# A two-layer graph network: edge tiles loaded and stored in pairs, and the copies into PSUM placed one by one in the step

## The chip, the cores and the metric

The kernel runs on one core of one Trainium2 chip. A core has five engines with instruction streams of their own: TensorE (PE in the profile, PEld for its weight loads), VectorE (DVE), ScalarE (ACT), GpSimd (POOL) and SyncE (SP). Each works through its stream in order and waits on semaphores for the others. Data goes between memory and the core's SBUF through DMA queues; here SyncE issues the plain loads and stores, and GpSimd issues gathers by row number. The metric is the device time of one launch in microseconds (us). The times given are medians of a few runs; beside them stands one execution taken by the hardware profiler.

## The reference

There are 6250 nodes and 106250 edges with vectors of D = 256 float32 numbers. The edges are sorted by their destination `dst`. Two layers follow each other, each one wrapped in a residual and a layer normalisation:

```python
# layer 0
msg = relu(x[src] + edge_attr)
h   = x + x + segment_sum(msg, dst)
f   = gelu(bn1(h) @ W1.T + b1) @ W2.T + b2
x   = layernorm(x + bn2(h + f))
# layer 1
m   = gelu((x[src] + edge_attr) @ W1m + b1m) @ W2m + b2m
agg = segment_sum(m, dst) / max(degree, 1)
u   = gelu(agg @ W1u + b1u) @ W2u + b2u
x   = layernorm(x + layernorm(x + u))
```

The BatchNorms `bn1` and `bn2` use given means and variances.

## The kernel before

**What is computed when.** The product in layer 1 is split: (x[src] + edge) @ W1m is proj[src] + edge @ W1m, with proj = x @ W1m + b1m made per node at the end of layer 0. Layer 1 so gathers rows of proj where layer 0 gathers rows of x. The edges stand in 831 tiles of 128, eight tiles make a span, and a span has two groups of four tiles; there are V = 104 spans. In layer 1 all edge tiles have to be multiplied by W1m. For group 1 this is done in layer 1 itself. For group 0 it is done ahead, in layer 0, and the products z go to a buffer `zst` in memory, from which layer 1 loads them.

**The steps.** The program is one long list in an order written out by hand (`manual_schedule`), so each engine's stream is what the text of the program says, in that order. It has one step for each span v. While span v is gathered, span u = v-1 gets its edges added, span w = v-2 is summed into slots, and span v-3 (`full`) is added into node blocks. A step of layer 0 (`step_0`) has:

- `load_0(v+3)`: one load of the eight edge tiles of a span (1 MB, L774), and the node rows xb when a block begins (L1049);
- `gather`: eight indirect DMAs (L791) on GpSimd, one for each tile, into `ring[v % 5]`, the room that the span five before had; a gather waits until that span's slot sums (L874) have read the room;
- `turned`, twice: two edge tiles of group 0 are transposed on TensorE (L804) into a PSUM buffer `workP`, and ScalarE copies them to SBUF as `eaT` (L809);
- `one_hots(u)`: eight small comparisons on VectorE (L852);
- `full_0`: sums over slots are multiplied into the accumulators of the node blocks (L902), and the degrees are made (L910 on TensorE, L915 on VectorE);
- `activated(w, 1)`: the activation of group 1 on ScalarE (L843);
- `lifted` and `add_to_gathered`, four times: ScalarE copies two edge tiles from SBUF to a `workP` buffer (L828, called the lift here), and VectorE adds them to the gathered rows in the ring (L835);
- two `product`s (L817), each of two tiles by W1m; VectorE copies them to `z` (L1098 and L1107), and one store of 512 KB takes both to `zst` (L1108);
- `slot_nodes` (L861), `into_slots` (L874, TensorE: the sums over 32 slots into the one buffer `slotP`) and `kept_slots` (L883, ScalarE);
- one phase each of the node work that is under way (`advance`), the oldest block early in the step, the others at its end.

A step of layer 1 (`step_1`) is the same in build. It loads 512 KB of `zst` (L1226) and 512 KB of edges (L774) ahead, and x1 and degrees of a block when it begins; it transposes and multiplies group 1 of span u, adds these products from PSUM (L835), and lifts and adds the two pairs of group 0. When a node block begins, `full_1` first makes an opening one-hot on VectorE (L896), for which L902 waits. The node work of layer 1 is `nodes_1` (L1161 on TensorE, L1166 on VectorE, L1171 on ScalarE, L1188, L1198 and L1202, and the store L1210).

**Buffers.** There are four `workP` buffers, taken in turn by every transposition, lift and product, whichever engine fills them; a new use waits until the use four before has been read. The pool `edges` has four buffers `ea` of a whole span, and two of `z`. `slotP` has one buffer, which L915 reads last. The order of a layer-0 step before, in uses of `workP`: transpose 1, transpose 2, lift and add 1, lift and add 2, product 1, lift and add 3, lift and add 4, product 2. In layer 1: transpose 1, transpose 2, lift and add 1, lift and add 2, product 1 (added: the third add), product 2 (the fourth add).

Of the kernel before, what the change touches and what calls it, by code (L numbers as in the profile page):

```python
# [14 lines left out]
P = 128  # L15
D = 256
# [486 lines left out]
def kernel(  # L503
# [76 lines left out]
    zst = dram.tile([len(window), P, G * D], F32, name="zst")  # L580
# [52 lines left out]
    with (  # L633
        tc.tile_pool(name="check", bufs=1) as check,
        tc.tile_pool(name="state", bufs=1) as state,
        tc.tile_pool(name="edges", bufs=AHEAD + 1) as ep,
# [132 lines left out]
        def load_edges(v, some, to):  # L769

            counts = sum((tiles_of(v, g) for g in some), [])
            for j, k, n in runs(counts):
                r0 = (v * SPAN + some[0] * G + j) * P
                nc.sync.dma_start(  # L774
                    out=to[:n, j:k, :],
                    in_=edge_attr[r0 : r0 + (k - j - 1) * P + n, :].rearrange(
                        "(j p) d -> p j d", p=n
                    ),
                )

        def edge_tiles(v):
            ea = ep.tile([P, SPAN, D], F32, name="ea")
            for g in range(GROUPS):
                eas[v, g] = ea[:, g * G : (g + 1) * G, :]
            return ea
# [12 lines left out]
        def turned(v, g, q, ea):  # L798

            pair = tiles_of(v, g)[q : q + 2]  # L800
            pe = work().rearrange("p j (k e) -> p j k e", k=KC)
            for j, n in enumerate(pair):
                for k in range(KC):
                    nc.tensor.transpose(  # L804
                        pe[:, j, k, :n], ea[:n, q + j, k * P : (k + 1) * P], ident[:n, :n]
                    )
# [16 lines left out]
        def lifted(v, g, q, of):  # L823

            pair = tiles_of(v, g)[q : q + 2]
            ps = work()
            for j, k, n in runs(pair):
                nc.scalar.copy(ps[:n, j:k, :], of[:n, q + j : q + k, :])  # L828
# [212 lines left out]
        eas, xbs, acc, degs = {}, {}, {}, {}  # L1041

        def load_0(v):
            load_edges(v, range(GROUPS), edge_tiles(v))
# [30 lines left out]
        zs = {}  # L1075

        def step_0(v):
# [3 lines left out]
            if v < V:  # L1081
                gather(v, x)
                first = turned(v, 0, 0, eas[v, 0])
                second = turned(v, 0, 2, eas[v, 0])
                zs[v] = ep.tile([P, G, D], F32, name="z", bufs=2)
# [7 lines left out]
            if 0 <= u < V:  # L1093
                add_to_gathered(u, 0, 0, lifted(u, 0, 0, eas[u, 0]))
                add_to_gathered(u, 0, 2, lifted(u, 0, 2, eas[u, 0]))
            advance(early)
            if v < V:
                nc.vector.tensor_copy(zs[v][:, 0:2, :], product(*first))  # L1098
            if 0 <= u < V:
                for q in range(0, len(tiles_of(u, 1)), 2):  # L1100
                    add_to_gathered(u, 1, q, lifted(u, 1, q, eas[u, 1]))
                activated(u, 0, AF.Relu)
            if 0 <= w < V:
                slot_nodes(w)
                kept_slots(w, into_slots(w, D + 1))
            if v < V:
                nc.vector.tensor_copy(zs[v][:, 2:4, :], product(*second))  # L1107
                nc.sync.dma_start(out=zst[v], in_=zs.pop(v).rearrange("p j d -> p (j d)"))  # L1108
# [105 lines left out]
        def load_1(v):  # L1214
# [10 lines left out]
            edge_tiles(v)  # L1225
            nc.sync.dma_start(out=eas[v, 0].rearrange("p j d -> p (j d)"), in_=zst[v])  # L1226
            load_edges(v, [1], eas[v, 1])
# [9 lines left out]
        def step_1(v):  # L1237
# [5 lines left out]
            some = 0 <= u < V  # L1243
            if some:
                first = turned(u, 1, 0, eas[u, 1])
                second = turned(u, 1, 2, eas[u, 1])
# [4 lines left out]
            if 0 <= w < V:  # L1251
                activated(w, 1, AF.Gelu)
            if some:
                add_to_gathered(u, 0, 0, lifted(u, 0, 0, eas[u, 0]))
                add_to_gathered(u, 0, 2, lifted(u, 0, 2, eas[u, 0]))
# [12 lines left out]
        for v in range(AHEAD):  # L1268
            load_0(v)
# [7 lines left out]
        for v in range(AHEAD):  # L1277
            load_1(v)
# [66 lines left out]
```

## Time and profile before

| what | value |
|---|---|
| median of 3 runs | 2827.88 us (2816.51 to 2832.43) |
| profiled execution | 2846.84 us |
| its span on the core | 2845.0 us |
| mean granted TensorE clock | 0.869 of full speed |
| layer 0: first to last gather | about 5 to 1304 us |
| layer 1: first to last step | about 1440 to 2790 us |
| bytes through queue q1 (loads and stores of SyncE) | 309.65 MB, 32.3% of 16 engines' span |
| bytes through queue q0 (gathers) | 217.71 MB, 25.1% |

How to read the lines that follow: times are in us unless marked ns. In the groups of instructions a line names the code line, engine, operation, output <- input and the number of instructions; then busy time and mean ns of one; then the idle time of the engine just before them and what ended most of it. In a timeline a line is start, duration, engine, code line and tile names, and in brackets the idle time ahead of it and the releaser ("remote" is a semaphore update of another engine that the profile doesn't trace to one instruction; "issue" is time in which nothing shown was waited for). In the list of waits: who waited <- for what: us in all, times, longest. Matmuls are pipelined and their ends are modelled.

### The profile page before, as it was taken

How to read it: one execution, taken by the hardware profiler on the slowest of the kernel's cores; microseconds unless marked ns; L12 is line 12 of the kernel's file. 1: busy time of each engine (PE TensorE's matmuls, PEld its weight loads, DVE VectorE, ACT ScalarE, POOL GpSimd, SP SyncE). 2: the span in 40 equal slices, each digit the busy share in tenths (PEclk: the TensorE clock that was granted, in tenths of full speed). 3: DMA queues.
4: the chain of work that ended last, by engine and by line, in shares of the span. 5: the costliest groups of instructions: out<-in, count | busy, mean ns of one | idle time of the engine just before them, and what ended most of it. 6: DMA issues, size and time to landing. Idle time of an engine off the chain costs nothing.

```text
span 2845.0 us, 37182 instructions
## 1 busy us (share of the span) xinstructions
PE 2074.6 (73%) x11784; PEld 1530.3 (54%) x11784; DVE 1410.2 (50%) x4130; ACT 1347.7 (47%) x2140; POOL 1579.9 (56%) x1671
## 2 busy tenths in 40 slices
PE   3788887887887787788357766776677677757776
PEld 2556655665665565565235544554555556545554
DVE  3554555555555555555124544455455455545555
ACT  1455555555554554555123544445444454435443
POOL 6556565665656665562455554555555656555540
PEclk7998999999998998998668987888888889878887
DMA  6676676676776776774445554555555555545540
GB/s 213 223 233 218 217 242 215 230 240 206 239 228 209 233 235 214 234 226 157 125 137 163 180 169 140 166 168 172 170 165 183 171 167 188 173 147 165 170 131 14
DMA packets 312069, 531.71 MB, mean 187 GB/s; under 512 B 36325, under 2 KB 231480, under 8 KB 311736
## 3 DMA queue, kind: packets, MB, share of 16 engines
q1 hardware_dynamic: 231416, 309.65, 32.3%
q0 software_dynamic: 79744, 217.71, 25.1%
q8 instruction: 97, 1.59, 0.2%
q10 hardware_dynamic: 704, 1.87, 0.2%
q14 instruction: 108, 0.88, 0.1%
HBM read 455.34 MB, written 73.75 MB: 186 GB/s over the span
## 4 chain that ended last, share of the span: by engine, by line
PE 25%; another core or an unknown queue 12%; issue 7%; DVE 6%; ACT 5%; DMA 2%; POOL 0%; ACTq 0%; DVEq 0%; SPq 0%; POOLq 0%
PE workP L817 10%; PE nodeP L1188 3%; PE slotP L874 3%; PE acc L902 3%; PE workP L804 2%; PE nodeP L1161 2%; DVE ring L835 2%; DMA ring<-proj,src_sb 1%; ACT ring L843 1%; ACT L958 1%; ACT workP L828 1%; DVE hot L852 1%; ACT eaT L809 1%; DVE uT L1166 1%
## 5 line engine op out<-in xcount | busy, mean ns | idle before, releaser
L791 POOL DMA_INDIRECT ring<-proj,src_sb x831 | 789.8, 950 | 671.2 <-issue 303.8
L791 POOL DMA_INDIRECT ring<-in_x_dram,src_sb x831 | 788.2, 949 | 513.3 <-issue 224.0
L817 PE MATMUL workP<-w1m_sb,eaT 128*128 128x256 f32 x3324 | 905.7, 416 | 146.7 <-ACT eaT L809 88.8
L835 DVE TENSOR_TENSOR ring<-workP,ring 128x512 f32<-128x512 f32 x832 | 542.7, 682 | 622.5 <-remote 322.3
L817 PEld LDWEIGHTS workP<-w1m_sb,eaT 128*128 128x128 f32 x3324 | 656.8, 206 | 354.7 <-issue 128.7
L902 PE MATMUL acc<-hot,sums 128*128 128x160 f32 (+19 forms) x1360 | 264.5, 332 | 303.3 <-DVE hot L896 169.2
L843 ACT ACTIVATE ring<-ring 128x1024 f32<-128x1024 f32 x418 | 441.9, 1058 | 75.8 <-DVE ring L835 65.2
L902 PEld LDWEIGHTS acc<-hot,sums 128*128 128x128 f32 x1360 | 210.8, 217 | 343.1 <-DVE hot L896 125.2
L828 ACT COPY workP<-ea 128x512 f32<-128x512 f32 x624 | 344.2, 595 | 93.7 <-DVE ring L835 62.1
L883 ACT COPY sums<-slotP 128x257 f32<-128x257 f32 (+1 forms) x208 | 76.9, 370 | 641.0 <-remote 324.5
L804 PE MATMUL workP<-ident,ea 128*128 128x128 f32 x1662 | 258.0, 293 | 158.5 <-DVE z L1098 105.6
L809 ACT COPY eaT<-workP 128x512 f32<-128x512 f32 x416 | 228.9, 585 | 296.2 <-PE workP L804 148.0
L874 PE MATMUL slotP<-ring,hot 128*32 128x257 f32 (+1 forms) x3324 | 265.5, 402 | 91.5 <-remote 40.3
L804 PEld LDWEIGHTS workP<-ident,ea 128*128 128x128 f32 x1662 | 205.4, 150 | 222.2 <-DVE z L1098 131.1
L852 DVE TENSOR_SCALAR hot<-ramp,slot 128x32 f32<-128x32 f32 x1662 | 265.8, 257 | 0.0
L874 PEld LDWEIGHTS slotP<-ring,hot 128*32 128x32 f32 x3324 | 108.5, 112 | 221.6 <-issue 105.5
L1098 DVE COPY z<-workP 128x512 f32<-128x512 f32 x104 | 71.3, 685 | 201.2 <-remote 128.0
L1171 ACT ACTIVATE uT<-uT,cols_sb 128x256 f32<-128x256 f32 (+1 forms) x100 | 44.9, 495 | 255.9 <-DVE uT L1166 214.0
L915 DVE TENSOR_TENSOR degs<-degs,slotP 1x160 f32<-1x160 f32 (+24 forms) x170 | 36.4, 241 | 226.8 <-issue 69.6
L1161 PE MATMUL nodeP<-fT,w 128*128 128x256 f32 (+1 forms) x400 | 105.6, 408 | 23.3 <-issue 11.6
L1188 PE MATMUL nodeP<-w2u_sb,uT 128*128 128x256 f32 (+1 forms) x392 | 106.1, 432 | 5.8 <-DVE y L1202 5.0
L1161 PEld LDWEIGHTS nodeP<-fT,w 128*128 128x128 f32 x400 | 80.6, 209 | 43.8 <-issue 21.3
(112 smaller groups left out, 1466.2 us busy)
## 6 DMA issues: line engine op xcount, KB each, us to landing
ea<-in_edge_attr_dram SPq DMA_DIRECT2D x103, 1024.0 KB
zst<-z SPq DMA_DIRECT2D x104, 512.0 KB
ea<-zst SPq DMA_DIRECT2D x104, 512.0 KB
ea<-in_edge_attr_dram SPq DMA_DIRECT2D x103, 512.0 KB
ring<-in_x_dram,src_sb POOLq DMA_INDIRECT x831
ring<-proj,src_sb POOLq DMA_INDIRECT x831
xb<-in_x_dram SPq DMA_DIRECT2D x24, 256.0 KB
x1d<-x SPq DMA_DIRECT2D x24, 256.0 KB
```

Of the source, the lines that this page charges most:

```text
L791: nc.gpsimd.indirect_dma_start(out=rings[v % RING][:n, g * G + j, :D], out_offset=None, in_=table, in_offset=bass.IndirectOffsetOnAxis(ap= ...
L804: nc.tensor.transpose(pe[:, j, k, :n], ea[:n, q + j, k * P : (k + 1) * P], ident[:n, :n])
L809: nc.scalar.copy(eaT[:, j:k, :, :n], pe[:, j:k, :, :n])
L817: nc.tensor.matmul(ph[:n, j, :], lhsT=eaT[:, j, k, :n], rhs=w1m_sb[:, k, :], start=(k == 0), stop=(k == KC - 1),)
L828: nc.scalar.copy(ps[:n, j:k, :], of[:n, q + j : q + k, :])
L835: nc.vector.tensor_add(r[:n, at + j : at + k, :D], ps[:n, j:k, :], r[:n, at + j : at + k, :D])
L843: nc.scalar.activation(at, at, func)
L852: nc.vector.tensor_scalar(hots[v][:n, j, :], ramp[:n, :SLOTS], slot[:n, t : t + 1], None, op0=ALU.is_equal,)
L874: nc.tensor.matmul(ps[q * SLOTS : (q + 1) * SLOTS, :width], lhsT=hot[:n, j, :], rhs=r[:n, j, :width], start=(i == 0), stop=(i == PAIR - 1 ...
L902: nc.tensor.matmul(acc[b][:, k, cols], lhsT=its[:, k * P : (k + 1) * P], rhs=at, start=(begins and k == 0), stop=(last_span[b] == v and k ...
L1161: nc.tensor.matmul(ps[:, o - i, :width], lhsT=w12[:, k, o * P : (o + 1) * P], rhs=mT[:, k, :width], start=(k == 0), stop=(k == KC - 1),)
L1188: nc.tensor.matmul(ps[:n, h, :], lhsT=uT[:, k, h * P : h * P + n], rhs=w2u_sb[:, k, :], start=(k == 0), stop=(k == UC - 1),)
```

## The change

Edge tiles are handled in pairs throughout. The pool `edges` has 16 buffers of two tiles where it had four of eight, and `z` has four of two tiles where it had two of four. A load is one pair (256 KB), and in layer 0 each of the two products is stored by itself as soon as it is copied (256 KB; `zst` is laid out for that). The load of a pair is issued right behind the lift that frees a pair's room, four spans ahead (`raised`), where before a whole span was loaded at the head of the step, three spans ahead. At the start of both layers four spans are loaded ahead, not three.

The lifts and their adds are moved. In layer 0 the order in uses of `workP` is now: transpose 1, lift and add 1, transpose 2, lift and add 2, product 1, lift and add 3, lift and add 4, product 2; the one-hots come after the first add, the second lift after `activated(w, 1)`, the third behind the first product, and the fourth behind `activated(u, 0)`. In layer 1: transpose 1, lift and add 1, transpose 2, lift and add 2, product 1, product 2. What is computed stays the same.

```diff
--- before.py
+++ after.py
@@ -577,7 +577,7 @@
     proj = dram.tile([N, D], F32, name="proj")
     x1d = dram.tile([N, D], F32, name="x1d")
     degd = dram.tile([1, N], F32, name="degd")
-    zst = dram.tile([len(window), P, G * D], F32, name="zst")
+    zst = dram.tile([len(window), G // 2, P, 2 * D], F32, name="zst")
 
     c.update(
         ident=ident, ones=ones, eps=eps, col=col, row=row, src_sb=src_sb, dstf=dstf,
@@ -633,7 +633,7 @@
     with (
         tc.tile_pool(name="check", bufs=1) as check,
         tc.tile_pool(name="state", bufs=1) as state,
-        tc.tile_pool(name="edges", bufs=AHEAD + 1) as ep,
+        tc.tile_pool(name="edges", bufs=(AHEAD + 1) * SPAN // 2) as ep,
         tc.tile_pool(name="hots", bufs=2) as hp,
         tc.tile_pool(name="nodes", bufs=2) as npool,
         tc.tile_pool(name="accP", bufs=2, space=bass.MemoryType.PSUM) as psa,
@@ -766,23 +766,27 @@
             nc.sync.dma_start(out=b2m_col, in_=b2m.rearrange("o (k p) -> p (o k)", p=P))
 
 
-        def load_edges(v, some, to):
-
-            counts = sum((tiles_of(v, g) for g in some), [])
-            for j, k, n in runs(counts):
-                r0 = (v * SPAN + some[0] * G + j) * P
+        eas = {}
+        HALVES = [(g, q) for g in range(GROUPS) for q in range(0, G, 2)]
+
+        def edge_tile(v, g, q):
+            eas[v, g, q] = ep.tile([P, 2, D], F32, name="ea")
+            return eas[v, g, q]
+
+        def load_edges(v, g, q):
+
+            pair = tiles_of(v, g)[q : q + 2]
+            if v >= V or not pair:
+                return
+            to = edge_tile(v, g, q)
+            for j, k, n in runs(pair):
+                r0 = (v * SPAN + g * G + q + j) * P
                 nc.sync.dma_start(
                     out=to[:n, j:k, :],
                     in_=edge_attr[r0 : r0 + (k - j - 1) * P + n, :].rearrange(
                         "(j p) d -> p j d", p=n
                     ),
                 )
-
-        def edge_tiles(v):
-            ea = ep.tile([P, SPAN, D], F32, name="ea")
-            for g in range(GROUPS):
-                eas[v, g] = ea[:, g * G : (g + 1) * G, :]
-            return ea
 
         def gather(v, table):
             for g in range(GROUPS):
@@ -795,14 +799,15 @@
                         in_offset=bass.IndirectOffsetOnAxis(ap=src_sb[:n, t : t + 1], axis=0),
                     )
 
-        def turned(v, g, q, ea):
-
+        def turned(v, g, q):
+
+            ea = eas[v, g, q]
             pair = tiles_of(v, g)[q : q + 2]
             pe = work().rearrange("p j (k e) -> p j k e", k=KC)
             for j, n in enumerate(pair):
                 for k in range(KC):
                     nc.tensor.transpose(
-                        pe[:, j, k, :n], ea[:n, q + j, k * P : (k + 1) * P], ident[:n, :n]
+                        pe[:, j, k, :n], ea[:n, j, k * P : (k + 1) * P], ident[:n, :n]
                     )
             eaT = hp.tile([P, 2, KC, P], F32, name="eaT", bufs=3)
             for j, k, n in runs(pair):
@@ -820,12 +825,13 @@
                     )
             return ph
 
-        def lifted(v, g, q, of):
-
+        def lifted(v, g, q):
+
+            of = eas[v, g, q]
             pair = tiles_of(v, g)[q : q + 2]
             ps = work()
             for j, k, n in runs(pair):
-                nc.scalar.copy(ps[:n, j:k, :], of[:n, q + j : q + k, :])
+                nc.scalar.copy(ps[:n, j:k, :], of[:n, j:k, :])
             return ps
 
         def add_to_gathered(v, g, q, ps):
@@ -1038,10 +1044,9 @@
             )
             nc.sync.dma_start(out=rows_of(proj, b), in_=y[:n, :H, :])
 
-        eas, xbs, acc, degs = {}, {}, {}, {}
+        xbs, acc, degs = {}, {}, {}
 
         def load_0(v):
-            load_edges(v, range(GROUPS), edge_tiles(v))
             for b in range(blocks):
                 if first_span[b] == v:
                     _, H, n = shape(b)
@@ -1072,7 +1077,11 @@
             for b in into_blocks(v, acc, opened_0, degs):
                 begun(b, nodes_0(b, acc.pop(b), xbs.pop(b), degs.pop(b)))
 
-        zs = {}
+        def stored(v, q, ps):
+
+            z = ep.tile([P, 2, D], F32, name="z", bufs=4)
+            nc.vector.tensor_copy(z, ps)
+            nc.sync.dma_start(out=zst[v, q // 2], in_=z.rearrange("p j d -> p (j d)"))
 
         def step_0(v):
             u, w, full = v - 1, v - 2, v - 3
@@ -1080,9 +1089,17 @@
                 load_0(v + AHEAD)
             if v < V:
                 gather(v, x)
-                first = turned(v, 0, 0, eas[v, 0])
-                second = turned(v, 0, 2, eas[v, 0])
-                zs[v] = ep.tile([P, G, D], F32, name="z", bufs=2)
+                first = turned(v, 0, 0)
+
+            def raised(g, q):
+
+                if 0 <= u < V and tiles_of(u, g)[q : q + 2]:
+                    add_to_gathered(u, g, q, lifted(u, g, q))
+                    load_edges(u + AHEAD + 1, g, q)
+
+            raised(0, 0)
+            if v < V:
+                second = turned(v, 0, 2)
             if 0 <= u < V:
                 one_hots(u)
             early, late = running[:1], running[1:]
@@ -1090,22 +1107,19 @@
                 full_0(full)
             if 0 <= w < V:
                 activated(w, 1, AF.Relu)
-            if 0 <= u < V:
-                add_to_gathered(u, 0, 0, lifted(u, 0, 0, eas[u, 0]))
-                add_to_gathered(u, 0, 2, lifted(u, 0, 2, eas[u, 0]))
+            raised(0, 2)
             advance(early)
             if v < V:
-                nc.vector.tensor_copy(zs[v][:, 0:2, :], product(*first))
+                stored(v, 0, product(*first))
+            raised(1, 0)
             if 0 <= u < V:
-                for q in range(0, len(tiles_of(u, 1)), 2):
-                    add_to_gathered(u, 1, q, lifted(u, 1, q, eas[u, 1]))
                 activated(u, 0, AF.Relu)
+            raised(1, 2)
             if 0 <= w < V:
                 slot_nodes(w)
                 kept_slots(w, into_slots(w, D + 1))
             if v < V:
-                nc.vector.tensor_copy(zs[v][:, 2:4, :], product(*second))
-                nc.sync.dma_start(out=zst[v], in_=zs.pop(v).rearrange("p j d -> p (j d)"))
+                stored(v, 2, product(*second))
             advance(late)
 
 
@@ -1222,9 +1236,12 @@
                         out=degs_1[b][:, :width],
                         in_=degd[:, b * SB : b * SB + width].to_broadcast([P, width]),
                     )
-            edge_tiles(v)
-            nc.sync.dma_start(out=eas[v, 0].rearrange("p j d -> p (j d)"), in_=zst[v])
-            load_edges(v, [1], eas[v, 1])
+
+        def load_products(v, q):
+            if v < V:
+                nc.sync.dma_start(
+                    out=edge_tile(v, 0, q).rearrange("p j d -> p (j d)"), in_=zst[v, q // 2]
+                )
 
         def opened_1(b):
             acc_1[b] = psa.tile([P, KC, SB], F32, name="acc")
@@ -1241,18 +1258,27 @@
             if v < V:
                 gather(v, proj)
             some = 0 <= u < V
+
+            def raised(q):
+                if some:
+                    add_to_gathered(u, 0, q, lifted(u, 0, q))
+                    load_products(u + AHEAD + 1, q)
+
             if some:
-                first = turned(u, 1, 0, eas[u, 1])
-                second = turned(u, 1, 2, eas[u, 1])
+                first = turned(u, 1, 0)
+            raised(0)
+            if some:
+                load_edges(u + AHEAD + 1, 1, 0)
+                second = turned(u, 1, 2)
                 one_hots(u)
             early, late = running[:1], running[1:]
             if 0 <= full:
                 full_1(full)
             if 0 <= w < V:
                 activated(w, 1, AF.Gelu)
+            raised(2)
             if some:
-                add_to_gathered(u, 0, 0, lifted(u, 0, 0, eas[u, 0]))
-                add_to_gathered(u, 0, 2, lifted(u, 0, 2, eas[u, 0]))
+                load_edges(u + AHEAD + 1, 1, 2)
             advance(early)
             if some:
                 add_to_gathered(u, 1, 0, product(*first))
@@ -1265,8 +1291,11 @@
             advance(late)
 
         begin()
-        for v in range(AHEAD):
-            load_0(v)
+        for v in range(AHEAD + 1):
+            for g, q in HALVES:
+                load_edges(v, g, q)
+            if v < AHEAD:
+                load_0(v)
         load_w(w1t_sb, w1t)
         load_w(w2t_sb, w2t)
         slots_of_edges()
@@ -1274,8 +1303,12 @@
         for v in range(V):
             step_0(v)
             beside.get(v, lambda: None)()
-        for v in range(AHEAD):
-            load_1(v)
+        for v in range(AHEAD + 1):
+            if v < AHEAD:
+                load_1(v)
+            for q in (0, 2):
+                load_products(v, q)
+                load_edges(v, 1, q)
         for v in range(V, V + 3):
             step_0(v)
         finish()
```

## The prediction

> **What bounds the kernel now.** I read the page's busy times first, then the groups of instructions, the list of waits, and the timeline of single steps. All sums are against the profiled execution (2846.84 us, span 2845.0); the three timed runs have a median of 2827.88, 0.7% under it, so a difference found in the one is carried to the other unscaled. From no change, a measurement of this kernel can tell about 0.5% (14 us).
>
> ```profile
> PE 2074.6 (73%) x11784; PEld 1530.3 (54%) x11784; DVE 1410.2 (50%) x4130; ACT 1347.7 (47%) x2140; POOL 1579.9 (56%) x1671
> ...
> L791 POOL DMA_INDIRECT ring<-proj,src_sb x831 | 789.8, 950 | 671.2 <-issue 303.8
> L791 POOL DMA_INDIRECT ring<-in_x_dram,src_sb x831 | 788.2, 949 | 513.3 <-issue 224.0
> ```
>
> No engine is full. POOL issues 8 gathers in a step, 0.95 us each with 0.30 between: 8 x 0.95 + 7 x 0.30 = 9.7 us. Yet the median step, from one copy of the slot sums (L883) to the next, is 12.3 us in layer 0 and 12.2 in layer 1. The timeline of a layer-0 step shows the rest:
>
> ```profile
> 613.12 1.89 PE L817 MATMUL workP<-w1m_sb,eaT 128*128 128x256 f32 x8
> ...
> 614.95 1.08 PE L874 MATMUL slotP<-ring,hot 128*32 128x257 f32 x16
> ...
> 618.45 0.95 POOL L791 DMA_INDIRECT ring<-in_x_dram,src_sb  x1 [0.30 <-issue]
> 620.42 0.69 DVE L1098 COPY z<-workP 128x512 f32<-128x512 f32 x1 [4.84 <-remote]
> ...
> 621.43 0.38 ACT L883 COPY sums<-slotP 128x257 f32<-128x257 f32 x1 [4.16 <-remote]
> 621.86 0.95 POOL L791 DMA_INDIRECT ring<-in_x_dram,src_sb  x1 [2.47 <-ACT sums L883]
> ```
>
> The first product ends at 615.01 and the slot sums at 616.03 by the record, but VectorE and ScalarE move on only at 620.42 and 621.43, after the last gather of the batch ended at 619.40. The next batch starts 2.47 later (median of layer 0: 2.58). This is how the trace has it throughout: what TensorE finishes late in a batch of gathers is seen by the other engines after the batch. Of the degree products (L910) of layer 0, those that ended under 4.5 us after a batch began held VectorE's L915 up by over 1 us in 13 of 56 steps, those that ended later in 35 of 38. So layer 0 is a loop: batch 9.7, gap 2.6, together 12.3. TensorE's own end of the slot sums lies a median 3.2 us before the copy: that is the slack of everything else. In 21% of the steps it is under 0.7.
>
> Layer 1 has a mean step of 13.34 against its median of 12.23. The difference sits in 19 stalls: two batches 0.3 apart, then POOL idle for 9 to 13 us. One of them:
>
> ```profile
> 1824.32 0.95 POOL L791 DMA_INDIRECT ring<-proj,src_sb  x1 [0.30 <-issue]
> 1825.50 0.69 DVE L835 TENSOR_TENSOR ring<-workP,ring 128x512 f32<-128x512 f32 x1 [11.40 <-remote]
> 1828.36 0.87 DVE L1166 SCALAR_TENSOR_TENSOR uT<-degb,b,nodeP 128x256 f32<-128x256 f32 x2 [2.17 <-remote]
> 1828.87 0.91 ACT L1171 ACTIVATE uT<-uT,cols_sb 128x256 f32<-128x256 f32 x2 [12.19 <-DVE uT L1166]
> 1829.15 1.25 DVE L852 TENSOR_SCALAR hot<-ramp,slot 128x32 f32<-128x32 f32 x8
> 1829.68 1.05 ACT L809 COPY eaT<-workP 128x512 f32<-128x512 f32 x2
> 1830.31 0.35 DVE L896 TENSOR_SCALAR hot<-ramp,node_of 128x256 f32<-128x256 f32 x1
> ...
> 1830.71 2.08 PE L902 MATMUL acc<-hot,sums 128*128 128x256 f32 x4 [13.19 <-DVE hot L896]
> ...
> 1836.90 0.94 POOL L791 DMA_INDIRECT ring<-proj,src_sb  x1 [11.64 <-ACT ring L843]
> ```
>
> The slot sums of the step before ended 3.8 us after the earlier batch had begun, early enough to get through, so the next batch followed at once and the second product and L1161 were held over both. In 10 of the 19 stalls a new node block opens (L896 in the gap), and TensorE waits for it:
>
> ```profile
> PE acc L902 <- DVE hot L896: 169.2, 20, 48.2
> ```
>
> **The change, part by part.** *Transfers.* A step of layer 0 has 4 loads and 2 stores of 256 KB for one load of 1 MB and one store of 512 KB; layer 1 has 4 loads of 256 KB for 2 of 512 KB. Bytes are the same, and runs of 2 KB move as fast as those of 4 KB (85 and 177 ns a packet in the trace, 24.0 and 23.2 GB/s an engine). SyncE issues one in 0.33 to 0.47 us:
>
> ```profile
> 607.65 0.37 SPq L774 DMA_DIRECT2D ea<-in_edge_attr_dram  x1
> ...
> 608.47 0.46 SPq L1015 DMA_DIRECT2D x1d<-x  x1
> ```
>
> Six of them are 2.4 us of a 12.3 us step on an engine with nothing else. What landed shows the next price: the 1 MB load issued at 607.65 had moved by 612.80, the 256 KB store issued behind it at 608.47 by 613.62, 0.8 us after it, which is about its own bytes. The Trainium skill, "DMA: Bandwidth & Descriptors" (section "Anatomy of one DMA"), gives each DMA some 2.0 us of fixed cost beside its bytes, and half efficiency at about 860 KB; it fits this on POOL's kind of DMA. That speaks against the change: 4 more DMAs a step are 8 us, 104 x 8 = +832 us in layer 0, if they stood one behind the other on the path. By the row they overlap in the queue; I take the row. And they aren't on the path: an edge tile is loaded 3 to 4 steps (37 to 49 us) ahead of its transpose and lands 2 to 6 us after issue. Even at 10 us late the cover holds. SyncE's queue is now held at each lift, in turn, and the x1d, proj and output stores queue behind it; they have no reader in the same layer. Price 0; without that cover each late load would stop TensorE at L804 for what it is late.
>
> *Start and turn of the layers.* The first tile is there after 256 KB, not 1 MB: TensorE's first transpose, at 13.38 us waiting for this load, may come some 3 us earlier. But the second product copy is at 57.19 because five batches of gathers run to 57. Price 0 (-3 to 0). A fourth span loaded ahead: 0.
>
> *Order, layer 0.* The four workP buffers go round in the order of use. The second transposes (T2) used to wait for the third add of the step before, now for the fourth: 0.68 later on VectorE, and T1 covers a part. After the release VectorE does z copy and two adds, ending 2.0 us later, where T2 could begin at 1.3 to 1.4: +0.55 us for T2, L902, L910, L817. The slack of 3.2 hides it in most steps. Two places don't: L910 ends later, and VectorE's L915 frees the one slotP buffer for L874. Of 94 steps 7 had L910 at 5.5 to 6.0 us after the batch began; those past 6.0 had steps about 1.3 us longer: 7 x 1.3 = +9. If all of it showed, 104 x 0.55 = +57. In return the first add no longer stands behind L915 (0.68 us of VectorE's work in the held steps): a bound of 21% x 104 x 0.68 = -15. I take +8, near the first since the release, not VectorE, ends those waits.
>
> *Order, layer 1, opening steps.* VectorE's first add now comes before the one-hots (L852) and L896, and it needs the first lift, which ScalarE does after the first transposes' copy. In the stall above: L1171 ends 1829.78, copy 0.59 to 1830.24 as now, lift 0.59 to 1830.8, add 0.69 to 1831.4, one-hots to 1832.7, L896 to 1833.0. L902 starts there instead of 1830.71: +2.3 us, and behind it on TensorE stand the product, L874 and, for it, POOL. 10 stalls x 2.3 = +23. Bounds: add alone 0.7 x 10 = 7; all 25 openings, 57. Other steps have 3.9 us of median slack: 0.
>
> *Order, layer 1, other stalls.* T2 now waits for the third add (0.69) that stands at the head after a release: +0.4 for L874. On the path in 9 stalls: +4. But the same 0.4 to 0.6 moves L874's end in the early batches, and 5 of 17 such ends lay at 5.2 to 5.6 us after the batch began; the ones not followed at once start at 5.6. Each stall costs 11.1 (mean idle) - 2.6 (usual gap) - 2.3 (gap saved before) = 6.2 us. Escapes: 0 to 5; I take 2, -12, since ends of 6.1 to 6.9 also got through.
>
> **Sum.** 8 + 23 + 4 - 12 = +23 us, about 0.8%: 2827.88 + 23 = 2851. No engine gains or loses an instruction beside SyncE.
>
> **The rivals.** *The stalls dissolve (faster).* Place: L874 in layer 1 after a short step; the delay of T2, and of activation L843 behind the lift, pushes its release past the early window, and POOL waits as in layer 0, where no batch but one followed at once. For it: ends cluster at 3.6 to 5.7. Against: 7 of the 17 are at 4.2 or less, and 0.6 doesn't carry them over. It decides from about 6 stalls gone (37 against the 35 of the other terms). Half of 19 gone: 9 x -6.2 = -56, the other layer-1 terms halved to 14, layer 0 +8: 2794; all gone: 2718.
>
> *Nothing moves.* The new waits end before the gathers do, the transfers were hidden before and after: 2828. For it: median slacks of 3.2 and 3.9 us. Against: L902's wait for L896 has no slack.
>
> *TensorE's chain becomes the loop.* T2's wait shows in each step: +57 in layer 0, 104 x 0.45 = +47 in layer 1, +23: 2955; a half of it, 2900. Against: steps with slack under 0.7 are a fifth.
>
> **How the numbers follow.** The sum as worked 0.42 (own range 2835 to 2880); stalls dissolve 0.32; nothing moves 0.16; TensorE's chain 0.10. Faster by over 0.5% (under 2813.7): 0.30 + 0.02 = 0.32. Within: 0.05 + 0.02 + 0.11 = 0.18. Slower (over 2842.0): 0.37 + 0.03 + 0.10 = 0.50. Range 2765 to 2900: it takes in the half-dissolved case and half of TensorE's chain.
>
> **What would show it.** Transfers: no wait of L804 or L828 for a DMA; SyncE's waits end at lifts. Layer 0: POOL's gap stays near 2.6 and the step near 12.3; L915's held waits grow. Openings: the wait of L902 for the opening one-hot above 169 us, L902 about 7.3 us after a double batch instead of 5.1. Stalls: their number near 17 to 19. I am wrong if the number of double batches falls below about 13, if gathers cost other than 0.95 us among smaller transfers, or if TensorE is seen waiting for loads.

## The result and the profile after

The changed kernel takes 2912.68 us (median of 4 runs) against 2830.15 for the kernel before: 1.029 times as long, 95% interval 1.0245 to 1.0343. It is slower, as forecast, but by 82 us where 23 were forecast, and 2912.68 lies above the range of 2765 to 2900.

First the groups of GpSimd's gathers (busy us, mean ns of one, then the idle time ahead of them), layer 1 above layer 0. The line L791 is now L795.

```profile
L795 POOL DMA_INDIRECT ring<-proj,src_sb x831 | 791.3, 952 | 682.0 <-issue 379.2
L795 POOL DMA_INDIRECT ring<-in_x_dram,src_sb x831 | 789.3, 950 | 563.9 <-issue 349.0
```

A gather costs what it did. GpSimd's idle time has grown by 51 us in layer 0 (513.3 before) and by 11 in layer 1 (671.2). Counted by steps, the time from the first to the last copy of slot sums is 1320 us in layer 0 (1269 before) and 1376 in layer 1 (1357): +51 and +19. The prediction had +8 and +15. The step of layer 0 has a median of 13.3 us, up from 12.3.

The groups of instructions name the place. Of the changed kernel (L921 is the degree add, L880 the slot sums):

```profile
L921 DVE TENSOR_TENSOR degs<-degs,slotP 1x160 f32<-1x160 f32 (+24 forms) x170 | 36.2, 240 | 358.4 <-remote 259.3 <-PE workP L822 59.3 <-issue 25.3
L880 PE MATMUL slotP<-ring,hot 128*32 128x257 f32 (+1 forms) x3324 | 284.9, 426 | 237.1 <-remote 175.9 <-issue 43.6 <-DVE degs L921 9.5
```

The same two groups of the kernel before:

```profile
L915 DVE TENSOR_TENSOR degs<-degs,slotP 1x160 f32<-1x160 f32 (+24 forms) x170 | 36.4, 241 | 226.8 <-issue 69.6 <-remote 65.2 <-PE workP L817 59.7
L874 PE MATMUL slotP<-ring,hot 128*32 128x257 f32 (+1 forms) x3324 | 265.5, 402 | 91.5 <-remote 40.3 <-PE workP L817 24.4 <-issue 23.1
```

VectorE's idle time ahead of the degree add grew from 226.8 to 358.4 us. TensorE's ahead of the slot sums (of both layers), which need the one `slotP` buffer that the add frees, grew from 91.5 to 237.1. The timeline of a step of the changed kernel shows both waits:

```profile
776.49 0.95 POOL L795 DMA_INDIRECT ring<-in_x_dram,src_sb  x1 [2.69 <-issue]
...
778.17 0.67 DVE L1083 COPY z<-workP 128x512 f32<-128x512 f32 x1
...
779.37 1.38 PE L809 MATMUL workP<-ident,ea 128*128 128x128 f32 x8
...
782.39 0.43 PE L916 MATMUL slotP<-hot,sums 128*1 128x161 f32 x2
...
785.25 0.94 POOL L795 DMA_INDIRECT ring<-in_x_dram,src_sb  x1 [0.30 <-issue]
788.04 0.37 DVE L921 TENSOR_TENSOR degs<-degs,slotP 1x125 f32<-1x125 f32 x2 [4.53 <-remote]
...
788.51 1.19 PE L880 MATMUL slotP<-ring,hot 128*32 128x257 f32 x16 [3.76 <-remote]
...
789.87 0.95 POOL L795 DMA_INDIRECT ring<-in_x_dram,src_sb  x1 [3.68 <-issue]
```

The degree product ends at 782.82, 6.3 us after the batch began. VectorE sees it at 788.04, 1.8 us after the last gather's end (786.19). Only then do the slot sums run, and only after them the next batch: 3.68 us of idle GpSimd in place of 2.6, and a period of 13.4.

### The profile page after: what moved, and what is told of

It is laid out like the page before. It is cut to its first block, busy times and chain, and to the rows that moved or that the text cites. A ratio compares the mean times of both kernels' runs of the same rounds, so it can differ in the third digit from the quotient of the medians.

```text
span 2913.1 us, 39112 instructions
## 1 busy us (share of the span) xinstructions
PE 2069.1 (71%) x11784; PEld 1554.9 (53%) x11784; DVE 1419.4 (49%) x4130; ACT 1343.2 (46%) x2140; POOL 1582.5 (54%) x1671
## 4 chain that ended last, share of the span: by engine, by line
PE 52%; another core or an unknown queue 19%; issue 10%; DVE 10%; ACT 6%; DMA 2%; POOL 0%; ACTq 0%; DVEq 0%; SPq 0%; POOLq 0%
PE workP L822 22%; PE slotP L880 7%; PE acc L908 6%; PE workP L809 5%; PE nodeP L1202 3%; DVE ring L841 3%; PE nodeP L1175 2%; DVE hot L858 2%; PE nodeP L1037 1%; ACT ring L849 1%; ACT workP L834 1%; PE nodeP L1004 1%; PE nodeP L991 1%; PE slotP L916 1%
## 5 line engine op out<-in xcount | busy, mean ns | idle before, releaser
L795 POOL DMA_INDIRECT ring<-proj,src_sb x831 | 791.3, 952 | 682.0 <-issue 379.2
L795 POOL DMA_INDIRECT ring<-in_x_dram,src_sb x831 | 789.3, 950 | 563.9 <-issue 349.0
L822 PE MATMUL workP<-w1m_sb,eaT 128*128 128x256 f32 x3324 | 931.7, 427 | 113.1 <-ACT eaT L814 57.5
L841 DVE TENSOR_TENSOR ring<-workP,ring 128x512 f32<-128x512 f32 x832 | 562.7, 684 | 701.0 <-remote 290.4
L822 PEld LDWEIGHTS workP<-w1m_sb,eaT 128*128 128x128 f32 x3324 | 681.3, 214 | 331.2 <-issue 111.8
L908 PE MATMUL acc<-hot,sums 128*128 128x160 f32 (+19 forms) x1360 | 255.1, 324 | 285.0 <-DVE hot L902 145.2
L880 PE MATMUL slotP<-ring,hot 128*32 128x257 f32 (+1 forms) x3324 | 284.9, 426 | 237.1 <-remote 175.9
L814 ACT COPY eaT<-workP 128x512 f32<-128x512 f32 x416 | 243.4, 585 | 309.5 <-PE workP L809 171.9
L834 ACT COPY workP<-ea 128x512 f32<-128x512 f32 x624 | 365.8, 593 | 0.0
L880 PEld LDWEIGHTS slotP<-ring,hot 128*32 128x32 f32 x3324 | 127.2, 116 | 356.7 <-remote 193.4
L921 DVE TENSOR_TENSOR degs<-degs,slotP 1x160 f32<-1x160 f32 (+24 forms) x170 | 36.2, 240 | 358.4 <-remote 259.3
L1083 DVE COPY z<-workP 128x512 f32<-128x512 f32 x208 | 142.1, 683 | 134.7 <-PE workP L822 51.8
```

Of the source, the lines that this page charges most:

```text
L795: nc.gpsimd.indirect_dma_start(out=rings[v % RING][:n, g * G + j, :D], out_offset=None, in_=table, in_offset=bass.IndirectOffsetOnAxis(ap= ...
L814: nc.scalar.copy(eaT[:, j:k, :, :n], pe[:, j:k, :, :n])
L822: nc.tensor.matmul(ph[:n, j, :], lhsT=eaT[:, j, k, :n], rhs=w1m_sb[:, k, :], start=(k == 0), stop=(k == KC - 1),)
L834: nc.scalar.copy(ps[:n, j:k, :], of[:n, j:k, :])
L841: nc.vector.tensor_add(r[:n, at + j : at + k, :D], ps[:n, j:k, :], r[:n, at + j : at + k, :D])
L880: nc.tensor.matmul(ps[q * SLOTS : (q + 1) * SLOTS, :width], lhsT=hot[:n, j, :], rhs=r[:n, j, :width], start=(i == 0), stop=(i == PAIR - 1 ...
```

## The experiments

The runs came in four groups of four and one of two, each group on a chip of its own: the kernel before took 2780, 2197, 2835, 2843 and 2789 us on the five chips. Ratios are therefore always to the kernel before on the same chip. For the traces I give two spans, from the first to the last slot copy of each layer, and how many of 97 steps of layer 0 had slot sums that started within 0.9 us of the degree add ("tied"). A span is that of one execution: the same program for layer 0 took 1269 and 1281 us in two kernels on one chip, so a difference of 10 or 20 us between two spans says little by itself.

**First theory.** In layer 0 the new order of lifts makes the degree product late, its release is held, and the slot sums wait. Rival A: the many small transfers cost. Rival B: the opening steps of layer 1, which the prediction priced, carry most of it.

**Old order, new transfers.** The lifts of both layers go back to their old places; loads and stores stay pairs. (Shown is the first lift of layer 0; the fourth and those of layer 1 are moved back in the same way.)

```diff
+                second = turned(v, 0, 2)          # layer 0, ahead of the lifts again
-            raised(0, 0)
             ...
                 activated(w, 1, AF.Relu)
+            raised(0, 0)
             raised(0, 2)
```

> The changed kernel with the lifts of both layers back in the old order; loads and stores stay pairs of tiles. Theory (the degree product of layer 0 ends too late in a batch of gathers, its release is held, the slot sums wait for the slotP buffer): the order is the cause, so 2830 +-14 us, layer-0 step back at a median of 12.3. Rival A (the smaller transfers cost): 2895 to 2915, layer-0 step still 13.3.

Three of four runs took 2830 to 2833 us and one 2785, beside 2780 for the kernel before, so no clear verdict. In its trace, of a run of 2830, the layer-0 step was 12.2 and 51 steps tied. There is no trace of the kernel before on this chip, so where the 50 us over 2780 lie isn't known.

**Old order in layer 1 only.**

```diff
-            raised(0)                             # layer 1
             ...
                 activated(w, 1, AF.Gelu)
+            raised(0)
             raised(2)
```

> The changed kernel with the old order in layer 1 only. Theory: the loss is made in layer 0, some 55 of 83 us, so 2880 to 2895; layer-0 step 13.3, layer-1 mean step back at 13.3. Rival B (the opening steps of layer 1, which the prediction sized at +23, carry most of it): 2850 or less.

1.015 (1.004 to 1.025).

**Old order in layer 0 only** (the first experiment's edit, layer 1 as changed).

> The changed kernel with the old order in layer 0 only. Theory: 2845 to 2855, layer-0 step 12.3, layer-1 mean 13.5. Rival A (transfers): over 2880. Rival B: 2885 or more.

1.022 (1.011 to 1.032). The expectations stood on 2830 us and this chip had 2780. As ratios, the first theory asked for 1.018 to 1.023 in the run ahead of this one and for 1.005 to 1.009 here. It got 1.015 and 1.022: the second is a miss, in the range of rivals A and B. The opening one-hot came 7.5 us after a double batch (mean of 9), against 5.2 in the kernel with the old layer-1 order on the same chip (mean of 11).

**Second transposes ahead of the first lift** (old order in layer 1).

```diff
                 first = turned(v, 0, 0)
+                second = turned(v, 0, 2)
             raised(0, 0)
-            if v < V:
-                second = turned(v, 0, 2)
```

> As the kernel with the old order in layer 1 only, and in layer 0 the second transposes ahead of the first lift again, so that they wait for the third add of the step before and not the fourth; the other lifts stay where the change put them. If the buffer turn of the second transposes pushes the degree product over the edge: under 2850, layer-0 step 12.3. If it is the place of the first add ahead of the one-hots, or the lifts between the products: still 2880 to 2895.

1.014 (1.005 to 1.024), as with the old order in layer 1 alone (1.015). So "under 2850", on a chip with 2780, decides nothing; beside its neighbour, and within the 1% either way of these intervals, the buffer turn of the second transposes has no effect that shows. That was the prediction's reason for the delay in layer 0.

**The kernels again, and the degree product moved.** The product and add of the degrees (L910, L915) leave the block sums of span v-3 and come right behind the second product, for span w = v-2. What is computed is the same.

```diff
-            if degs is not None:                  # in into_blocks
-                nc.tensor.matmul(rest[:, :span], ...)
-                ... nc.vector.tensor_add(to, to, ...)
 ...
                 stored(v, 2, product(*second))
+            if 0 <= w < V:
+                degrees(w)                        # the same product and add
             advance(late)
```

> The kernel before once more, beside the other three on one chip, for its trace there: the trace of before and those of the first four experiments come from different chips, and on the second chip the kernel before took 2780 us where it had taken 2830. All theories: ratio 1.00. If the layer-0 step here is still 12.3 with about 40 of 97 slot sums right behind the degree add, the 50 us between chips lie elsewhere; if it is lower, they are the same wait.

> The changed kernel on the same chip as its counterpart. Theory (held degree product in layer 0): 1.025 to 1.033 times the kernel before, two thirds of it in layer 0 (step 0.5 us longer). Rival A (transfers): the same ratio, but the loss is spread over both layers.

> The kernel before with the degree product and its add (L910, L915) moved from the block sums to right behind the second product of the step in which the slot sums were made, so that its release comes at the head of a batch of gathers and slotP is free early. Theory: no slot sums wait for the degree add any more; the held steps, some 40% of layer 0, lose 0.3 to 1 us each, so 1.2 to 3% less in layer 0, ratio 0.985 to 0.995. Rivals A and B: ratio 1.00.

> The changed kernel with the degree product moved in the same way. Theory: the loss of layer 0 is gone with the wait that made it; layer-0 step 12.3 or less, ratio to the kernel before 0.99 to 1.005, and within 0.5% of the kernel before with the same move but for layer 1. Rival A (transfers): still 1.02 or more.

On this chip all four kernels were much faster and nearly alike: 1.000 (0.999 to 1.002), 1.0012 (1.0004 to 1.0020), 0.9993 (0.9983 to 1.0003) and 1.0010 (1.0001 to 1.0019) of 2196.8 us. The page of the kernel before there:

```profile
span 2194.2 us, 37182 instructions
...
L791 POOL DMA_INDIRECT ring<-proj,src_sb x831 | 789.2, 950 | 305.2 <-issue 149.0
L791 POOL DMA_INDIRECT ring<-in_x_dram,src_sb x831 | 787.4, 948 | 256.3 <-issue 149.4
```

Gathers cost the same 0.95, but 0.30 x 830 = 249 us of the 256.3 is the space between two gathers: GpSimd hardly waits in layer 0. Of TensorE's semaphore updates all are in the trace within 0.15 us of the instruction's recorded end; in the first trace of the kernel before it is 36%, on the third chip 37%. Where releases arrive at once, the whole change costs 0.12% (some 2.5 us), although 47 of 104 steps of the changed kernel are tied there too (2 before). So a tied step isn't slow by itself; the loss goes with late releases. The granted TensorE clock was higher on this chip as well (0.95 in place of 0.87), and no run separates the two. This is the rival "nothing moves", on the chip where its premise holds.

**Third chip of the experiments, late releases again.** Both kernels once more, the first experiment's kernel, and the changed kernel with the degree product moved.

> The kernel before, for its trace beside the next three on one chip. On the chip of the four runs ahead of this, every engine's releases were seen at once (TensorE's 100% within 0.15 us, against 36% in the first trace), the kernel before took 2197 us, and the change cost 0.1%. If this chip delivers late again: 2770 to 2850. If it delivers at once: 2197.

> The changed kernel. Where releases come late: 1.02 to 1.035 of the kernel before. Where they come at once: 1.001, as before; then nothing in these four tells the theories apart.

> The changed kernel with the old order of lifts in both layers, as in the first experiment, where three of four times lay 1.8% above the kernel before and one 0.2%. Where releases come late: the theory (order alone) has 1.000 to 1.005, rival A (the many small transfers) 1.015 to 1.03, spread over both layers.

> The changed kernel with the degree product and add moved to right behind the second product of the step that made the slot sums. Where releases come late: the theory has 0.985 to 1.005 of the kernel before, layer-0 step 12.3 or less, and no slot sums right behind the degree add; rival A 1.015 or more.

| kernel | ratio (95%) | layer 0, us | layer 1, us | tied |
|---|---|---|---|---|
| before | 1.003 (0.999 to 1.006) | 1274 | 1346 | 39 |
| changed | 1.035 (1.028 to 1.042) | 1340 | 1380 | 84 |
| old order, new transfers | 1.012 (1.005 to 1.018) | 1326 | 1337 | 85 |
| changed, degrees moved | 1.012 (1.009 to 1.016) | 1279 | 1339 | 0 |

Two things follow. The wait is the cause in layer 0: with the degree product out of the way, and nothing else changed, no slot sums are tied to it, the layer-0 span falls from 1340 to 1279 (1274 before) and 2.3% of the 3.5% are gone. The same move leaves the kernel before at 1.000 (next group), so it is no gain of its own. The 1.012 that is left is above the range of the theory. Layer 1, whose program this move doesn't touch, is 41 us shorter in the last row's trace too; that execution took 2838 us, and the median is 2866. The last row's groups of gathers:

```profile
L795 POOL DMA_INDIRECT ring<-proj,src_sb x831 | 789.9, 951 | 648.5 <-issue 309.2
L795 POOL DMA_INDIRECT ring<-in_x_dram,src_sb x831 | 787.1, 947 | 524.4 <-issue 303.1
```

against the changed kernel on that chip:

```profile
L795 POOL DMA_INDIRECT ring<-proj,src_sb x831 | 788.6, 949 | 694.0 <-issue 358.4
L795 POOL DMA_INDIRECT ring<-in_x_dram,src_sb x831 | 787.1, 947 | 584.6 <-issue 352.1
```

But the first theory falls in its other half: the order isn't needed for it. The transfers alone, in the old order, cost 1.2%, tie 85 steps and lengthen layer 0 by 52 us in the trace. Rival A (1.015 to 1.03) is near in the size of its loss and wrong in the spread: layer 1 got no longer (1337 against 1346).

**Second theory.** Transfers and order each tip layer 0 towards the tied steps; the order costs in layer 1 by itself. Four parts, on a chip with 2843 us for the kernel before. In the first the kernel before gets the new order with whole loads and stores (shown is the first lift of layer 0, the others alike):

```diff
                 first = turned(v, 0, 0, eas[v, 0])
+            raised(0, 0)                          # lift and add, no load
+            if v < V:
                 second = turned(v, 0, 2, eas[v, 0])
```

> The kernel before with the new order of the lifts in both layers, and loads and stores whole as they were. With the transfers alone (1.012) and all of the change (1.035) it makes the third corner of a square. If order and transfers add up: 1.02 to 1.025. If the transfers are what tips layer 0, and the order costs only in layer 1: 1.005 to 1.015. If either alone tips layer 0 into the held steps: 1.02 to 1.03.

In the second each load of the kernel before is cut into DMAs of two tiles, at the old place:

```diff
-            for j, k, n in runs(counts):
+            for j, k, n in pieces:                # at most two tiles each
...
-            nc.sync.dma_start(out=eas[v, 0]..., in_=zst[v])
+            for q in (0, 2):
+                nc.sync.dma_start(out=eas[v, 0][:, q : q + 2, :]..., in_=zst[v][:, q * D : (q + 2) * D])
```

> The kernel before with each load of edges and of z cut into DMAs of two tiles, issued one behind the other at the old place; stores whole, order as before. If the number of loads is what the transfers cost: 1.008 to 1.018, late degree adds at 1.0 to 1.8 us after the batch instead of before its end. If it is their place behind the lifts, or the stores: 0.998 to 1.004.

In the third the store of a step is cut in two:

```diff
                 nc.vector.tensor_copy(zs[v][:, 0:2, :], product(*first))
+                nc.sync.dma_start(out=zst[v][:, : 2 * D], in_=zs[v][:, 0:2, :]...)
```

> The kernel before with the store of the products cut in two, the first issued right behind the first copy, which stands at the head of the release; loads and order as before. If the stores are what the transfers cost: 1.008 to 1.018. If not: 0.998 to 1.004.

The fourth moves the degree product in the kernel before.

> The kernel before with the degree product and add moved to behind the second product of the step of the slot sums. On a chip with late releases the theory has 0.985 to 0.998: no slot sums held by the degree add, layer-0 step at 12.3 or less. If the held steps of the kernel before cost nothing (their steps had 12.35 against 12.29): 1.000 to 1.005.

| kernel | ratio (95%) | layer 0, us | layer 1, us | tied |
|---|---|---|---|---|
| new order alone | 1.031 (1.024 to 1.037) | 1287 | 1416 | 51 |
| loads in pieces alone | 1.008 (1.004 to 1.011) | 1299 | 1354 | 71 |
| stores in two alone | 1.004 (1.001 to 1.007) | 1280 | 1348 | 35 |
| before, degrees moved | 1.000 (0.997 to 1.003) | 1269 | 1355 | 0 |

Loads and stores add up to 1.2%, which is what the transfers cost together; the place of the loads behind the lifts adds nothing that shows. The order alone costs 3.1%, a little above all three of the ranges given for it. Most of it lies in layer 1: 1416 us against 1348 and 1355 in the last two rows, whose layer 1 is that of the kernel before. In layer 0 it adds only 7 to 18 us to theirs. Order and transfers don't add up: 3.1 + 1.2 is more than the 2.9 and 3.5 measured for both. By the spans they do in layer 0 (52 for the transfers, 7 to 18 for the order, 51 and 66 for both) and don't in layer 1 (-9, 61 to 68, and 19 and 34 for both). The tied steps of the kernel before cost it nothing: without them it is as fast.

**The opening one-hot a step earlier.** To see whether the layer-1 part is the opening wait, L896 is computed right behind the slot numbers of the step before, out of VectorE's queue, in both kernels.

```diff
                 slot_nodes(w)
+                opening_nodes(w)                  # hot3 of a block that begins with w
 ...
-                    nc.vector.tensor_scalar(at, ramp[:, : hi - lo], ...)
+                    at = hot3s.pop(b)[:, : hi - lo]
```

> The kernel before with the opening one-hot of layer 1 (L896) made a step earlier, right behind the slot numbers, so that it is no longer behind the held add and the eight one-hots on VectorE. If the opening wait sets the length of the 6 to 14 opening stalls, as the prediction had it: each gets 2.3 us shorter (the product then waits for its transposes' copy, not for L902), so 14 to 32 us less, ratio 0.989 to 0.995. If the stalls only end otherwise: 0.998 to 1.002.

> The changed kernel with the opening one-hot made a step earlier. The change moved it to 7.0 to 7.5 us behind the double batch from 5.1; with the one-hot out of that queue the layer-1 part of the loss (19 to 34 us) should go: ratio to the kernel before 1.010 to 1.025 in place of 1.029 to 1.035, with layer 0 as slow as the change made it. If the opening wait isn't the cause of the layer-1 part: 1.03 or more.

0.995 (0.992 to 0.998) and 1.017 (1.011 to 1.023). The first is the fastest kernel found, faster than both, by 15 us of 2789. Its layer-1 span was 1296 us, and 13 stalls of over 6 us were left where the traces of before had 19 each. The second ratio lies in its range, but the traces don't give the reason that was forecast. With the move, layer 1 of the changed kernel took 1323 us. That is 53 and 57 less than without it on other chips, but the kernel before became some 50 to 60 us shorter there too, so 27 us between the two are left, where it was 19 and 34. What is smaller here is the loss of layer 0, which the move doesn't touch: 1288 against 1269, in place of 51 and 66. The changed kernel without the move didn't run on this chip, so what share of the loss the opening wait makes is not shown.

## Why the prediction was wrong

**What bounds the kernel: right.** Batches of gathers, late releases and the gap set the step; on the chip with prompt releases the same instructions took 21 to 23% less time.

**"Price 0" for the transfers: the step that failed.** The prediction asked whether data would come late, and beside the first load and the turn of the layers nothing waited for data. But the 624 more DMAs cost 1.2% by themselves, 33 us, or 0.05 us each, and in the trace 52 of the 66 us by which layer 0 grew on that chip. The Trainium skill's 2.0 us of fixed cost a DMA ("DMA: Bandwidth & Descriptors", "Anatomy of one DMA"), fitted on GpSimd's kind of DMA, gives an estimate of over 1200 us if it is added up for all of them. So the row was the better guide, but it was a row about landing. The loss is in late releases. Of 90 batches of layer 0 in each trace, the table counts the steps whose degree product ended 4.5 us or more after the batch began, and those of them whose degree add came 0.9 us or more after the batch's end:

| trace | late products | late degree adds |
|---|---|---|
| before, first chip | 39 | 14 |
| loads in pieces alone | 64 | 34 |
| all transfers alone, third chip | 70 | 52 |
| changed, first chip | 67 | 49 |
| changed, third chip | 78 | 64 |

In these traces a step with a late degree add has a median of 13.4 to 13.6 us, all the others 12.3 to 12.4: each such release costs 1.0 to 1.3 us, and their number makes most of the loss of layer 0. How more DMAs delay a release no run shows; that stays open. Within one trace, batches in which more DMAs were issued did not have the later releases.

**"I take +8" in layer 0: the right chain, for the wrong cause.** L910 later, L915 held, L874 behind it through `slotP`: this is the wait that carried the loss, and with the degree product out of the way the loss of layer 0 was gone. But it was priced for the order alone. The order's own part is indeed small, 7 to 18 us alone and 14 on top of the transfers; that the transfers work through the same wait was not in the sum. Nor is a step free of the one before, as the working with 7 steps that a shift of 0.55 us carries over an edge took it. In the kernel before, in the 58 steps whose degree product gets through, the transposes begin with the batch (median 0.02 us ahead of its start) and the product ends 3.3 us in. In the 32 held ones they begin 2.4 us in and it ends at 5.6, since slot sums and the second product still have to run when the batch begins. If the held release then comes after the batch, the next step starts late again. In the changed kernel late products (4.5 us and more) became the rule: 67 of 90 batches, 39 before. So 78 steps were tied, not 40 + 7. The bound of +57 "if all of it showed" is near the 51 and 66 by luck: it stood on the buffer turn of the second transposes, and undoing that had no effect that shows. The loss also differs by chip: where the kernel before took 2780 and 2789 us, layer 0 as the change has it took 1283 and 1288, with 21 and 23 such late releases.

**Layer 1: right in mechanism; the size isn't settled.** The timeline of an opening stall in the changed kernel:

```profile
1812.13 0.69 DVE L841 TENSOR_TENSOR ring<-workP,ring 128x512 f32<-128x512 f32 x1 [14.79 <-remote]
...
1813.44 0.91 ACT L1185 ACTIVATE uT<-uT,cols_sb 128x256 f32<-128x256 f32 x2 [6.60 <-DVE uT L1180]
1814.26 0.56 ACT L814 COPY eaT<-workP 128x512 f32<-128x512 f32 x1
1814.72 0.59 ACT L834 COPY workP<-ea 128x512 f32<-128x512 f32 x1
...
1815.35 0.69 DVE L841 TENSOR_TENSOR ring<-workP,ring 128x512 f32<-128x512 f32 x1 [1.54 <-ACT workP L834]
...
1815.95 1.25 DVE L858 TENSOR_SCALAR hot<-ramp,slot 128x32 f32<-128x32 f32 x8
...
1817.12 0.34 DVE L902 TENSOR_SCALAR hot<-ramp,node_of 128x256 f32<-128x256 f32 x1
...
1817.52 2.08 PE L908 MATMUL acc<-hot,sums 128*128 128x256 f32 x4 [9.32 <-DVE hot L902]
...
1825.34 0.94 POOL L795 DMA_INDIRECT ring<-proj,src_sb  x1 [14.42 <-ACT sums L889]
```

Activation, copy, lift, add, one-hots, opening one-hot, block sums stand in the order that the prediction wrote down. The wait for the opening one-hot in the changed kernel:

```profile
PE acc L908 <- DVE hot L902: 145.2, 12, 50.0
```

The sum isn't above 169 as I said it would be, because fewer waits lie in it (12, one of 50.0); without the longest one a wait is 95.2 / 11 = 8.7 us, before 121.0 / 19 = 6.4: 2.3 more, the predicted figure. In the stalls with an opening the block sums start 6.9 us behind the double batch (mean of 9 in this trace), 5.1 before (mean of 11), where the prediction had 7.3 and 5.1; GpSimd idles 14.3 us in these stalls in place of 12.0. With the +4, -12 and +23 the sum was +15; measured +19 in the first pair, +34 in the other. But the parts don't bear out the sum: the order alone made layer 1 61 to 68 us longer, and with the one-hot moved 27 us were left.

**The rivals.** The stalls didn't dissolve: 15 in place of 19 of over 6 us, and 28 batches of layer 1 followed at once in both. "Nothing moves" holds only on the chip with prompt releases. "TensorE's chain becomes the loop" came nearest in time (2900 for a half of it), by luck: the held release and not the transposes was the link.

## What to carry to other kernels

A wait with slack on average can be one of two rhythms of a loop (here steps of 12.3 and of 13.4 us), and then a small delay isn't priced by its length but by how many steps it moves to the slower rhythm; look at the steps with a late and with a timely release apart, and at what a step leaves to the next. A single-buffered tile (`slotP`) that a late consumer frees is where such a rhythm locked here; move the consumer to where its release arrives early, and do what depends on nothing ahead of the queue that is held up. Measure on more than one chip before a part is called free: here the same edit cost 0.1% on one and 3.5% on another.

## What the runs showed of the hardware

- The same kernel took 2197 us on one chip and 2780 to 2843 on the others. GpSimd's gathers were as long (0.95 us). The time from an instruction's recorded end to its semaphore update differed: it was within 0.15 us for all of TensorE's updates on the one, and for 34 to 51% in the traces of this kernel and its variants on the others. The mean granted TensorE clock was 0.94 to 0.95 on the one and 0.86 to 0.88 in the traces on the others; TensorE was busy 85% of the span on the one and 73% in the first trace. What makes the releases late there isn't in the profile.
- Held releases don't come at any time. Relative to the end of the batch of gathers the degree adds that waited came near -2.5, -1.8, -1.1, -0.4, 0.3, 1.0 and 1.7 us, some 0.7 us apart, and few came later than 1.95 (14 of some 900 in 14 traces). What sets these times isn't in the profile.
